# Placing a chunk's first DVE passes behind the scaling of transposes, and summing folded weights from PSUM, for three gates at once, with one copy no longer raised

## The chip, the cores and the metric

One core of one Trainium2 chip runs the whole program. The metric is the device time of one execution in microseconds (us). Several executions are quoted by their median, lowest and highest.

Names: TensorE (PE in the profile, PEld for its weight loads), VectorE (DVE), ScalarE (ACT), GpSimd (POOL), SyncE (SP, whose DMA issues are SPq). PSUM is the memory that TensorE writes to in this kernel, a bank one piece of it; SBUF is the memory of the other on-chip tiles.

Tiles in the profile: one unit of layer 0 makes, in this order, `pa` (adjacency times features), `ph` (times W1), `ps` (times W2) and `po` (adjacency again) in PSUM; `ag`, `hg`, `s` and `z` are what ACT makes of these four. `pT` is a transpose, `pf` a product of the fold, `parz` the first product of the loop of layer 3. A group such as `ps` stands for all its matmuls in one pass.

## The reference, cut to what matters

Four graph layers follow each other on `x` of shape (128, 64, 256) with one adjacency matrix of 64x64 per graph, each with a residual and a layer norm.

```python
# layer 0: five groups of nodes, two graph convolutions each (W1: 256->512, W2: 512->256)
x = _layernorm(x + _L0_gnn_ref(x, adj, W1, b1, W2, b2, fusion_w))
# layer 1: normalized adjacency, one matmul;  layer 2: polynomial in the row-normalized adjacency
x = _layernorm(x + _L1_gnn_ref(x, adj, W, b))
x = _layernorm(x + _L2_gnn_ref(x, adj, W, conv_w, conv_b))
# layer 3: five rounds of message passing and a GRU cell
x = _layernorm(x + _L3_gnn_ref(x, adj, nodemask, weight, w_ih, w_hh, b_ih, b_hh))

def _L3_gnn_ref(x, adj, mask, weight, w_ih, w_hh, b_ih, b_hh):
    A = (adj != 0).astype(x.dtype)
    h = x
    for l in range(5):
        m = jnp.einsum('bnd,de->bne', h, weight[l])
        agg = jnp.einsum('bij,bid->bjd', A, m)
        h = _gru_cell(agg, h, w_ih, w_hh, b_ih, b_hh)
    return h * mask[..., None]
```

## The kernel before

Layer 0 is worked in 16 units. While one unit multiplies, another is prepared: DVE builds a block-diagonal normalized adjacency `A`, TensorE transposes it into PSUM (`pT`), and DVE scales the transpose while it evicts it. The list `evictions` keeps these last scalings.

```python
        # prep(i), cut
                deg = small.tile([TR, w], F32, name="deg")
                nc.vector.tensor_reduce(deg[:r], av, AX.X, ALU.add)
                dinv = inv_sqrt(deg[:r], w, r, "d0")          # d0z, d0s on DVE; d0r on GpSimd; d0o on DVE
                nc.vector.tensor_mul(av, av, dinv[:, :, None].to_broadcast([r, w, u.n]))
                ...                                           # A0 = av * block, on DVE
                for t in range(ts.start, ts.stop):
                    nc.tensor.transpose(p[:r, t, :r], A0[:r, t, :r], ident[:r, :r])
                scale.append((AT[:r, ts, :r], p[:r, ts, :r], dinv[:, :, None].to_broadcast([r, w, r])))
            for v in scale:
                with tc.high_priority():
                    evictions.append(nc.vector.tensor_mul(*v))
```

Layers 1 and 2 take 8 graphs at a time (a chunk). Chunks 0 and 1 are woven into layer 0, the others into layer 3. A chunk's first stage reads the loaded adjacency `a64` twice, for `Ab` and for `rsum`; all the rest follows from these two.

```python
    def mid(c):
        a64 = adjs.pop(c)
        Ab = keep.tile([128, NP, 128], F32, name="Ab", bufs=1)
        nc.vector.tensor_mul(
            Ab.rearrange("p q (b m) -> p q b m", b=2),
            a64[:, :, None, :].to_broadcast([128, NP, 2, N]),
            pair[:, None, :, :].to_broadcast([128, NP, 2, N]),
        )
        A01 = keep.tile([128, NP, 128], F32, name="A01", bufs=4)
        nc.vector.tensor_scalar(A01, Ab, 0.0, None, op0=ALU.not_equal)
        rsum = small.tile([128, NP], F32, name="rsum")
        nc.vector.tensor_reduce(rsum, a64, AX.X, ALU.add)
        ...                                                   # rdeg, rinv, dinv1, dg from rsum
        nc.scalar.activation(poly, dg, AF.Identity, scale=cw[:, 2:3])
        ...
        yield
```

Between layer 0 and layer 3 the GRU's input weights are multiplied with each round's message weights (`pf`), and each product is split into the seven factors of a Strassen-like scheme (`V`; `WHH` for the hidden weights). Three copies on ACT and four sums on DVE belong to each product.

```python
    def factors(w, w21):
        nc.vector.tensor_add(w[:, 4, :], w21, w[:, 3, :])
        nc.vector.tensor_sub(w[:, 6, :], w[:, 0, :], w21)
        nc.vector.tensor_sub(w[:, 5, :], w[:, 4, :], w[:, 0, :])
        nc.vector.tensor_sub(w[:, 2, :], w[:, 1, :], w[:, 5, :])

    # fold(), cut: for each round l and gate q
                nc.scalar.copy(w[:, 0:2, :], p[:, :, 0:128])
                nc.scalar.copy(w[:, 3, :], p[:, 1, 128:256])
                v21 = ... work.tile([128, 128], F32, name="w21", bufs=3)
                nc.scalar.copy(v21, p[:, 0, 128:256])
                factors(w, v21)
                if l == 0:
                    factors(WHH[:, q], w21[:, q, :])

    # Chunk.state_of_layer2(k): the chunk's state transposed, first in the fold, later in the loop
            p = self.transpose(lambda q, k: self.xt[:, q, k * 128 : (k + 1) * 128], k, "pT3")
            with tc.high_priority():
                nc.scalar.copy(self.hT[:, k, :], p)
```

The build lays out each engine's queue. `tc.high_priority()` asks for an earlier place in it; `tc.issue_after(ins)` keeps an instruction behind `ins` in the queue (in the changed kernel `Ab` of chunk 0 runs at 174.69 us, behind the scaling at 169.20).

## Time and profile before

| | before |
|---|---|
| median of 3 runs | 2215.43 us (2214.81 to 2216.5) |
| profiled span | 2214.5 us, mean granted clock 0.994 |
| TensorE idle | 34.3 us, of which 15.1 us in one wait for `A` |

How to read it: TensorE is busy 98% of the span, so only what ends one of its few waits counts. The prediction shows the waits of TensorE, the timeline around the largest, and the windows with the clock. A number in square brackets at the end of a timeline line is how long the engine stood idle before that instruction, and what ended the idle time.

### The profile page before, as it was taken

How to read it: one execution, taken by the hardware profiler on the slowest of the kernel's cores; microseconds unless marked ns; L12 is line 12 of the kernel's file. 1: busy time of each engine (PE TensorE's matmuls, PEld its weight loads, DVE VectorE, ACT ScalarE, POOL GpSimd, SP SyncE). 2: the span in 40 equal slices, each digit the busy share in tenths (PEclk: the TensorE clock that was granted, in tenths of full speed). 3: DMA queues.
4: the chain of work that ended last, by engine and by line, in shares of the span. 5: the costliest groups of instructions: out<-in, count | busy, mean ns of one | idle time of the engine just before them, and what ended most of it. 6: DMA issues, size and time to landing. Idle time of an engine off the chain costs nothing.

```text
span 2214.5 us, 30166 instructions
## 1 busy us (share of the span) xinstructions
PE 2180.2 (98%) x11542; PEld 1911.4 (86%) x11542; DVE 1372.5 (62%) x3088; ACT 1003.1 (45%) x1853; POOL 571.0 (26%) x621
## 2 busy tenths in 40 slices
PE   9979999999999999999999999999999999999997
PEld 6657888888889889888889898888898898888886
DVE  3344666665766666666766676657666666566546
ACT  3233334445545454445454454455454544455453
POOL 3211122222222223223222222222222232232221
PEclk9989999999999999999999999999999999999999
DMA  5531210000100000000100010001000000000000
GB/s 166 178 109 55 58 46 4 1 3 1 41 1 4 1 20 22 3 1 7 35 1 3 1 41 1 3 1 41 1 1 1 20 10 1 1 10 11 1 1 20
DMA packets 54172, 51.12 MB, mean 23 GB/s; under 512 B 20878, under 2 KB 49036, under 8 KB 54028
## 3 DMA queue, kind: packets, MB, share of 16 engines
q1 hardware_dynamic: 49664, 43.96, 6.5%
q0 software_dynamic: 1936, 4.83, 0.8%
q8 instruction: 91, 1.49, 0.3%
q10 hardware_dynamic: 2428, 0.41, 0.1%
q14 instruction: 53, 0.43, 0.1%
HBM read 32.40 MB, written 16.78 MB: 22 GB/s over the span
## 4 chain that ended last, share of the span: by engine, by line
PE 94%; SPq 2%; DVE 1%; issue 1%; DMA 1%; ACT 0%; POOL 0%; POOLq 0%; DVEq 0%; ACTq 0%
PE parz L731 25%; PE pdrz L731 12%; PE pan L731 12%; PE pa L210 9%; PE pbrz L731 6%; PE pdn L731 6%; PE pT L772 4%; PE ps L442 4%; PE ph L426 3%; PE pbn L731 3%; PE pd L286 2%; PE pd L307 2%; SPq L362 1%; PE pa L411 1%; PE po L464 1%
## 5 line engine op out<-in xcount | busy, mean ns | idle before, releaser
L748 ACT COPY c<-parz 128x512 f32<-128x512 f32 x240 | 140.6, 586 | 322.4 <-PE parz L731 321.7
L731 PE MATMUL parz<-Th,WHH 128*128 128x256 f32 x960 | 286.0, 379 | 0.3 <-ACT c L748 0.3
L731 PE MATMUL parz<-Ta,V 128*128 128x256 f32 x960 | 285.8, 379 | 0.0
L711 POOL TENSOR_TENSOR Th<-hn 128x512 f32<-128x512 f32 x64 | 81.4, 1272 | 778.3 <-DVE hn L834 602.8
L831 ACT ACTIVATE NI<-NI,bih 128x512 f32<-128x512 f32 (+1 forms) x162 | 115.9, 715 | 206.0 <-DVE NI L826 205.8
L748 ACT COPY c<-pan 128x512 f32<-128x512 f32 x237 | 139.0, 586 | 150.1 <-PE pan L731 150.1
L731 PEld LDWEIGHTS parz<-Ta,V 128*128 128x128 f32 x960 | 182.5, 190 | 24.7
L731 PEld LDWEIGHTS parz<-Th,WHH 128*128 128x128 f32 x960 | 176.5, 191 | 21.1 <-ACT c L748 0.7
L803 ACT ACTIVATE RZ<-RZ,brz 128x512 f32<-128x512 f32 x160 | 116.0, 726 | 138.9 <-DVE RZ L760 138.9
L711 POOL TENSOR_TENSOR Ta<-agg 128x512 f32<-128x512 f32 x80 | 102.0, 1275 | 260.0 <-ACT agg L214 260.0
L760 DVE TENSOR_TENSOR RZ<-pdrz,c 128x512 f32<-128x512 f32 x80 | 55.0, 688 | 173.2 <-PE pdrz L731 173.2
L139 POOL TENSOR_TENSOR rs<-ve,mhalf 128x4 f32<-128x4 f32 (+3 forms) x67 | 68.9, 1029 | 298.3 <-DVE ve L137 234.4
L731 PE MATMUL pan<-Ta,V 128*128 128x256 f32 x474 | 141.3, 380 | 0.0
L731 PE MATMUL pan<-Th,WHH 128*128 128x256 f32 x474 | 141.1, 379 | 0.0
L754 DVE TENSOR_TENSOR NI<-pbn,c 128x512 f32<-128x512 f32 x79 | 54.6, 692 | 127.8 <-PE pbn L731 110.2
L210 PEld LDWEIGHTS pa<-A,h 128*128 128x128 f32 x1024 | 124.4, 192 | 3.3
L210 PE MATMUL pa<-A,h 128*128 128x128 f32 x1024 | 124.6, 275 | 0.0
L750 DVE TENSOR_TENSOR NI<-pdn,c 128x512 f32<-128x512 f32 x79 | 54.5, 689 | 112.7 <-ACT c L748 112.7
L832 DVE TENSOR_TENSOR RZ<-hn,NI 128x512 f32<-128x512 f32 (+1 forms) x129 | 87.8, 680 | 49.5 <-ACT NI L831 49.5
L834 DVE TENSOR_TENSOR hn<-RZ,NI 128x512 f32<-128x512 f32 (+1 forms) x161 | 109.8, 682 | 1.8
L833 DVE TENSOR_TENSOR RZ<-RZ 128x512 f32<-128x512 f32 (+1 forms) x161 | 109.5, 680 | 1.8
L442 PE MATMUL ps<-W,hg 128*125 128x256 f32 (+5 forms) x464 | 103.6, 380 | 0.3 <-ACT v L313 0.3
(220 smaller groups left out, 5077.0 us busy)
## 6 DMA issues: line engine op xcount, KB each, us to landing
out_dram<-xt SPq DMA_DIRECT2D x32, 256.0 KB
W<-in_w_dram SPq DMA_DIRECT2D x10, 512.0 KB
xt<-xb SPq DMA_DIRECT2D x32, 156.0 KB
xo<-in_x_dram SPq DMA_DIRECT2D x9, 512.0 KB
xb<-xo SPq DMA_DIRECT2D x9, 512.0 KB
xt<-xa SPq DMA_DIRECT2D x32, 100.0 KB
xg<-in_x_dram SPq DMA_DIRECT2D x25, 125.0 KB
xa<-xg SPq DMA_DIRECT2D x25, 125.0 KB
```

What stands on the lines that cost most here:

```text
L139: nc.gpsimd.tensor_tensor(rs[:r, :n], ve[:r, :n], mhalf[:r, :n], ALU.pow)
L210: nc.tensor.matmul(p[:, q * 128 : (q + 1) * 128], src[:, q, k * 128 : (k + 1) * 128], m[:, q, :], start=True, stop=True)
L442: nc.tensor.matmul(p[: u.rows[t], t - v, :], hg[:, e, u.off[t] : u.off[t] + u.rows[t]], W2[:, u.g, e, :], start=e == 0, stop=e == 3,)
L711: nc.gpsimd.tensor_sub(t[:, 0:2, :], a[:, :, H:], a[:, 0, :].rearrange("p (s n) -> p s n", s=2))
L731: nc.tensor.matmul(bank[:, g, :], w[:, q, i - 1, :], rhs, start=i in (1, 2, 5) and g == 0 and m == 0, stop=m == len(side) - 1, skip_group_ ...
L748: nc.scalar.copy(c, self.a)
L772: nc.tensor.transpose(p[:, q * 128 : (q + 1) * 128], src(q, k), ident)
L803: nc.scalar.activation(RZ[:, q, 0, :], RZ[:, q, 0, :], AF.Sigmoid, bias=b[0])
L831: nc.scalar.activation(n, n, AF.Tanh, bias=bih[:, 4 + j : 5 + j])
L832: e.tensor_sub(d, self.hT[:, j, f], n)
L833: e.tensor_mul(d, d, z)
L834: e.tensor_add(self.hn[:, j, f], d, n)
```

## The change

The intent: DVE should no longer reach `Ab` and `rsum` of the first chunk before their adjacency has landed. They are placed behind the most recent scaling of a transpose. In the fold, the sums with the fourth quarter of a product (`w21`) read it from the PSUM bank instead of a copy, the other sums of the three gates run in one instruction, and the copy of the transposed state (`hT`) loses its priority.

```diff
-        nc.vector.tensor_mul(
-            Ab..., a64..., pair...)
+        with tc.issue_after(evictions[-1].ins):
+            nc.vector.tensor_mul(
+                Ab..., a64..., pair...)
...
-        nc.vector.tensor_reduce(rsum, a64, AX.X, ALU.add)
+        with tc.issue_after(evictions[-1].ins):
+            nc.vector.tensor_reduce(rsum, a64, AX.X, ALU.add)
...
-    def factors(w, w21):
-        nc.vector.tensor_add(w[:, 4, :], w21, w[:, 3, :])
-        nc.vector.tensor_sub(w[:, 6, :], w[:, 0, :], w21)
-        nc.vector.tensor_sub(w[:, 5, :], w[:, 4, :], w[:, 0, :])
-        nc.vector.tensor_sub(w[:, 2, :], w[:, 1, :], w[:, 5, :])
+    def factors(w):
+        nc.vector.tensor_sub(w[:, :, 5, :], w[:, :, 4, :], w[:, :, 0, :])
+        nc.vector.tensor_sub(w[:, :, 2, :], w[:, :, 1, :], w[:, :, 5, :])
...
-                v21 = ... work.tile([128, 128], F32, name="w21", bufs=3)
-                nc.scalar.copy(v21, p[:, 0, 128:256])      # now for the last product alone
-                factors(w, v21)
-                if l == 0:
-                    factors(WHH[:, q], w21[:, q, :])
+                nc.vector.tensor_add(w[:, 4, :], p[:, 0, 128:256], w[:, 3, :])
+                nc.vector.tensor_sub(w[:, 6, :], w[:, 0, :], p[:, 0, 128:256])
+                if q == 2:
+                    factors(V[l])
+                if q == 2 and l == 0:
+                    nc.vector.tensor_add(WHH[:, :, 4, :], w21, WHH[:, :, 3, :])
+                    nc.vector.tensor_sub(WHH[:, :, 6, :], WHH[:, :, 0, :], w21)
+                    factors(WHH)
...
-            with tc.high_priority():
-                nc.scalar.copy(self.hT[:, k, :], p)
+            nc.scalar.copy(self.hT[:, k, :], p)
```

More of the change, by code (lines that the diff above doesn't have):

```diff
@@ L225, in mid @@
         Ab = keep.tile([128, NP, 128], F32, name="Ab", bufs=1)
-        nc.vector.tensor_mul(
-            Ab.rearrange("p q (b m) -> p q b m", b=2),
-            a64[:, :, None, :].to_broadcast([128, NP, 2, N]),
-            pair[:, None, :, :].to_broadcast([128, NP, 2, N]),
-        )
+        with tc.issue_after(evictions[-1].ins):
+            nc.vector.tensor_mul(
+                Ab.rearrange("p q (b m) -> p q b m", b=2),
+                a64[:, :, None, :].to_broadcast([128, NP, 2, N]),
+                pair[:, None, :, :].to_broadcast([128, NP, 2, N]),
+            )
         A01 = keep.tile([128, NP, 128], F32, name="A01", bufs=4)
@@ L675, in gnn_stack @@
     raw21 = []
-    def factors(w, w21):
-        nc.vector.tensor_add(w[:, 4, :], w21, w[:, 3, :])
-        nc.vector.tensor_sub(w[:, 6, :], w[:, 0, :], w21)
-        nc.vector.tensor_sub(w[:, 5, :], w[:, 4, :], w[:, 0, :])
-        nc.vector.tensor_sub(w[:, 2, :], w[:, 1, :], w[:, 5, :])
+    raw21 = []
+    def factors(w):
+        nc.vector.tensor_sub(w[:, :, 5, :], w[:, :, 4, :], w[:, :, 0, :])
+        nc.vector.tensor_sub(w[:, :, 2, :], w[:, :, 1, :], w[:, :, 5, :])
     def fold():
@@ L697, in fold @@
                 nc.scalar.copy(w[:, 3, :], p[:, 1, 128:256])
-                kept = l == L - 1 and q == 2
-                v21 = work.tile([128, 128], F32, name="kept21") if kept else work.tile([128, 128], F32, name="w21", bufs=3)
-                nc.scalar.copy(v21, p[:, 0, 128:256])
-                if kept:
+                if l == L - 1 and q == 2:
+                    v21 = work.tile([128, 128], F32, name="v21")
+                    nc.scalar.copy(v21, p[:, 0, 128:256])
                     raw21.append(v21)
-                factors(w, v21)
-                if l == 0:
-                    factors(WHH[:, q], w21[:, q, :])
+                nc.vector.tensor_add(w[:, 4, :], p[:, 0, 128:256], w[:, 3, :])
[6 more added lines that the diff above has]
+                    factors(WHH)
                 yield
```

## The prediction

> **What bounds the kernel now.** I read the page first (busy times, then the chain that ended last), then the waits of each engine, then the timeline around the two places where TensorE stood still.
>
> ```profile
> PE 2180.2 (98%) x11542; PEld 1911.4 (86%) x11542; DVE 1372.5 (62%) x3088; ACT 1003.1 (45%) x1853; POOL 571.0 (26%) x621
> PE 94%; SPq 2%; DVE 1%; issue 1%; DMA 1%; ACT 0%; POOL 0%; POOLq 0%; DVEq 0%; ACTq 0%
> ```
>
> The first line is the busy time of each engine in a span of 2214.5 us. TensorE is idle for 2214.5 - 2180.2 = 34.3 us in all. The change touches no matmul, so it can win from those 34.3 us and from slow clock, and from nothing else: 2% of 2215 us is 44 us, more than everything that is there. So the question is which part of the 34.3 us goes. The waits of TensorE say where most of it is (us in total, times, longest):
>
> ```profile
> PE pT L397 <- DVE A L389: 15.1, 1, 15.1
> PE pT L860 <- DVE hn L834: 4.1, 3, 1.6
> PE ph L426 <- ACT ag L416: 2.5, 1, 2.5
> PE pf L560 <- ACT w L700: 1.9, 1, 1.9
> PE pw L534 <- DVE zero L531: 1.5, 1, 1.5
> PE pa L411 <- DVE AT L401: 0.8, 1, 0.8
> ```
>
> One wait of 15.1 us holds nearly half. The rows pT L860 and pw L534 are the end and the start, which the change does not touch. From 350 to 2140 us, the long loop, TensorE has no gap (the windows view gives 1760.00 us of PE in the 1760 us from 380 to 2140). The timeline tells how the 15.1 us come about:
>
> ```profile
> 93.93 1.01 POOL L123 TENSOR_TENSOR d0r<-d0s,mhalf 126x4 f32<-126x4 f32 x1 [1.63 <-DVE d0s L121]
> 112.00 2.35 SPq L191 DMA_DIRECT2D a<-in_adj_dram  x2
> 119.25 0.69 DVE L226 TENSOR_TENSOR Ab<-a,pair 128x512 f32<-128x512 f32 x1 [25.46 <-DMA a<-in_adj_dram]
> 119.86 0.15 DVE L125 SCALAR_TENSOR_TENSOR d0o<-deg,d0r 126x4 f32<-126x4 f32 x1
> 120.68 0.75 DVE L389 TENSOR_TENSOR A<-ae,block 126x252 f32<-126x252 f32 x2
> 121.48 1.10 PE L397 MATMUL pT<-ident,A 126*126 126x126 f32 x4 [15.13 <-DVE A L389]
> 123.42 0.72 ACT L248 ACTIVATE poly<-dg,cw 128x512 f32<-128x512 f32 x1 [26.03 <-DVE dg L244]
> 124.65 0.65 ACT L416 COPY ag<-pa 128x264 f32<-128x264 f32 x2
> ```
>
> DVE works through a queue in order, and the queue has Ab of chunk 0 of the middle layers (L226, first used by TensorE at 213.69) in the middle of the preparation of layer 0's unit 7: behind d0s, ahead of d0o. The adjacency that Ab reads is issued by SP only at 112.00 and lands at 119.2. DVE stands for 25.46 us, d0o (its input from POOL was there at 94.94) and A wait behind, and TensorE, done with its work at 106.35, waits for A until 121.48. ACT has the same illness: poly, which needs dg of the same chunk, is ahead of ag, which makes the second wait (ph, 2.48 us). A third cost shows in the windows view (length, then PE, PEld, DVE, ACT, POOL busy, then clock, DMA share, GB/s):
>
> ```profile
> 100.00:106.00 6.00, 6.00 (x30) 5.20 (x28) 0.00 (x0) 0.00 (x0) 0.00 (x0) 1.00 0.40 96
> 115.00:120.00 5.00, 0.00 (x0) 0.00 (x0) 0.75 (x3) 0.00 (x0) 0.00 (x0) 0.50 0.43 111
> 125.00:127.00 2.00, 1.93 (x5) 1.52 (x6) 1.07 (x5) 1.27 (x4) 1.42 (x1) 0.50 0.43 160
> ```
>
> The granted clock is at half from 111 us until about 128, so that the first work after the stop also runs slow. The other place is the folding of weights, where TensorE waits 1.87 us:
>
> ```profile
> 323.32 0.58 ACT L780 COPY hT<-pT 128x512 f32<-128x512 f32 x1 [7.31 <-PE pT L772]
> 329.96 2.11 DVE L680 TENSOR_TENSOR WHH<-WHH,wh 128x128 f32<-128x128 f32 x2
> 338.18 1.99 PE L560 MATMUL pf<-ih,wl 128*128 128x256 f32 x8 [1.87 <-ACT w L700]
> ```
>
> hT, raised in priority, stands ahead of the fold's copies on ACT for 7.31 us while products from 317 us on are ready to be copied; and the sums on DVE, normally 0.28 us each, are stretched (two took 2.11).
>
> [...] L681 of 1.28 to 1.36 us ran beside L711 of POOL (1.37 us from 327.52). [...]
>
> **Part 1, Ab and rsum placed behind the last scaling of a transpose on DVE.** [...] By program order chunk 0's first stage is traced in the iteration after unit 11 was prepared, so Ab now follows AT of unit 11 (188.68 in the present trace), and chunk 1's follows AT of unit 14 (253.43). Both are far behind the landing at 119. So DVE runs d0o at 95, A by 96.5, and TensorE's transposes follow at 106 without a wait. What that is worth I take from the same work where it was not disturbed: unit 8 begins ps (32 matmuls of 256) at 150.23, pT at 157.24, ph (16 of 264) at 157.67, po at 161.24. That is 11.01 us from ps to po. In the disturbed pass ps begins at 99.18 and po at 130.22: 31.04 us. The difference is **20.0 us** (15.13 + 2.48 of waiting, some 2.4 of slow clock).
>
> Does the earlier work find its inputs? SP works off a backlog without a pause of note until 126, and that backlog does not move up. Unit 8's rows were issued by 96.5, needed at 148.31 - 20 = 128; unit 9's adjacency by 100.6, needed at 141.7 - 20 = 121.7; unit 10's by 119.1, needed at 160 - 20 = 140; unit 11's now waits for DVE and moves to about 126, needed at 153. All have 14 us or more, so I book no loss.
>
> What moves: about 3.5 us of DVE work for each of chunks 0 and 1. Chunk 0's has from about 169 to 193 (TensorE's transposes of Ab, 213.69 - 20). Chunk 1's has from 253.4 to 266.96 in present time, in which DVE has 3.9 us of plain idle before L314 and some gaps more. That fits narrowly, so I book **0.4 us** of new waiting around there.
>
> **Part 2, the fold.** Removed: 72 sums of 128x128 on DVE, 29 us busy in the trace (sum of L679 to L682) against 72 x 0.28 = 20 unblocked[...]; and 14 ACT copies of 0.28. Added: 30 sums with one input in PSUM, 128x128 (the PSUM form costs no more here: L754 0.69 against L832 0.68 at 512), and 14 sums of 128x384[...]. Measured start to start, 0.20 for the small (as 336.08 to 336.28)[...]. DVE gains little in plain time; it gains [...]that the ring of three w21 buffers, for which ACT waited 6.0 us, is gone. A bank is now held until DVE has read it, so DVE stays in TensorE's loop. I expect the wait of 1.87 to shrink to about 0.5: **1.4 us**.
>
> **Part 3, hT no longer raised.** In the fold it helps part 2. In the loop it happens 14 times; hT has some 14 us of other matmuls between its transposes and its first use by rz of the next step (eight products of 0.86 to 1.73 each), and an ACT copy in front costs 0.6 to 0.7 us. I book **0.2 us** lost.
>
> Sum: 2215.4 - 20.0 - 1.4 + 0.4 + 0.2 = **2194.6 us**.
>
> **The rivals.** (a) The wait is replaced: with DVE free, loads on the crowded SP queue hold TensorE up in 106 to 140 us. For it: SP issues without a break[...]. Against: the margins above. It would give back 3 to 10 us, 2198 to 2205. (b) The work put off collides with chunk 1's short window, or chunk 2's load, which SP must issue after Ab of chunk 0 has read its buffer, holds loads behind it in the SP queue. Against: the present trace has the same narrow order on a free DVE, and layer 0's loads are nearly all out by then. It would cost 1 to 6 us, about 2198. (c) Other order in the loop from ACT without the raised copies: a bank freed late, 14 times up to 0.5 us, 2200. (d) The fold's waits get worse, because a blocked large sum stands ahead of small ones that free banks: up to 3 us, 2197. A floor: 34.3 us idle plus 2.4 of slow clock, less some 12 us at the start and end: not under 2190.
>
> **Range and chances.** The trigger of the 20 us is plain and its removal certain, the rest is small on both sides, and rivals only lengthen: 2191 to 2202, with a tail upwards. Over 2% faster is out of reach (it needs 44 us), over 2% slower would need a new stall of 60 us, such as a queue in a bad order: 0.01 each way, 0.98 within.
>
> **What would show it.** Right: no wait of DVE for the adjacency, no row pT <- A and no ph <- ag among TensorE's waits, clock 1.00 between 110 and 128, PE busy lower by some 2 us with the same count, po of unit 5 near 110 and all later work 20 us earlier; Ab after 168; the row pf <- w gone, a smaller one to DVE in its place. Wrong: a new wait of TensorE of over 2 us before 200 (a), near 240 to 260 (b), at each change of chunk (c) or in the fold (d).

## The result, and the profile after

The changed kernel took 2195.51 us (median of 4 runs, 2195.18 to 2197.59), against 2215.97 us of the kernel before beside it (4 runs, 2214.81 to 2217.66). The ratio is 0.9909, 95% interval 0.9892 to 0.9926: within 2%. All ratios here are the mean time of one kernel's runs over that of the other's in the same rounds, so they are not quite the ratio of the medians.

Busy times of the engines, and the chain that ended last by engine, in the changed kernel:

```profile
PE 2177.2 (99%) x11542; PEld 1907.7 (87%) x11542; DVE 1362.9 (62%) x3060; ACT 1001.2 (46%) x1839; POOL 571.2 (26%) x621
PE 96%; DVE 1%; issue 1%; POOL 0%; ACT 0%; DMA 0%; SPq 0%; POOLq 0%; ACTq 0%; DVEq 0%
```

SPq, 2% of the chain before, is at 0%. TensorE idles 2193.5 - 2177.2 = 16.3 us instead of 34.3. Its waits in the changed kernel (us in total, times, longest), to be held against the rows that the prediction quotes:

```profile
PE pT L865 <- DVE hn L839: 4.1, 3, 1.6
...
PE pT L778 <- DVE V L705: 0.9, 1, 0.9
...
PE ph L428 <- ACT ag L418: 0.5, 1, 0.5
```

The rows of 15.1 and 2.5 us are gone (the 0.5 of ph lies at 12.39 us, at the start). In the fold, 0.9 us remain of 1.9. The same pass in the timelines, first of the kernel before and then of the changed kernel:

```profile
99.18 7.17 PE L442 MATMUL ps<-W,hg 128*126 128x256 f32 x32
...
130.22 1.95 PE L464 MATMUL po<-AT,s 126*128 126x126 f32 x16
```

```profile
95.54 0.16 DVE L125 SCALAR_TENSOR_TENSOR d0o<-deg,d0r 126x4 f32<-126x4 f32 x1 [1.19 <-POOL d0r L123]
95.95 0.75 DVE L391 TENSOR_TENSOR A<-ae,block 126x252 f32<-126x252 f32 x2
99.74 7.17 PE L444 MATMUL ps<-W,hg 128*126 128x256 f32 x32
106.75 0.60 PE L399 MATMUL pT<-ident,A 126*126 126x126 f32 x4
107.18 3.73 PE L428 MATMUL ph<-ag,W 128*128 128x264 f32 x16
110.75 1.95 PE L466 MATMUL po<-AT,s 126*128 126x126 f32 x16
111.80 2.25 SPq L191 DMA_DIRECT2D a<-in_adj_dram  x2
...
174.69 0.66 DVE L227 TENSOR_TENSOR Ab<-a,pair 128x512 f32<-128x512 f32 x1
```

The load is issued when it was before (111.80 against 112.00), but nothing stands behind it: `A` is built at 95.95, ten us before TensorE wants it, and `Ab` runs at 174.69, long after the landing and without a wait. The windows from 106 to 130 us (length, then busy time and count of PE, PEld, DVE, ACT, POOL, then clock, DMA share, GB/s), before and after:

```profile
106.00:130.00 24.00, 6.39 (x22) 4.74 (x21) 7.80 (x38) 4.29 (x9) 3.82 (x3) 0.64 0.49 150
```

```profile
106.00:130.00 24.00, 24.00 (x119) 17.09 (x118) 13.43 (x65) 10.05 (x18) 4.38 (x5) 1.00 0.51 163
```

TensorE is busy throughout and the clock stays at 1.00. From the starts of the same TensorE groups in both timelines the whole difference can be laid out, by stages (us; each is a difference of two starts in one timeline):

| stage | before | after | difference |
|---|---|---|---|
| span's start to ps of this pass | 99.18 | 99.74 | +0.56 |
| ps to po of this pass | 31.04 | 11.01 | -20.03 |
| po to the first product of the fold (pf) | 185.07 | 185.13 | +0.06 |
| fold: first pf to first matmul of the loop (parz) | 33.85 | 32.78 | -1.07 |
| loop: first parz to last transposes (pT) | 1856.66 | 1856.19 | -0.47 |
| last pT to the span's end | 8.69 | 8.69 | 0.00 |
| sum | 2214.48 | 2193.54 | -20.94 |

Such stages are free of the noise of the start and serve for the experiments too.

### The profile page after: what moved, and what is told of

It reads as the page before. It is cut to its first block, busy times and chain, and to the rows that moved or that the text cites.

```text
span 2193.5 us, 30145 instructions
## 1 busy us (share of the span) xinstructions
PE 2177.2 (99%) x11542; PEld 1907.7 (87%) x11542; DVE 1362.9 (62%) x3060; ACT 1001.2 (46%) x1839; POOL 571.2 (26%) x621
## 4 chain that ended last, share of the span: by engine, by line
PE 96%; DVE 1%; issue 1%; POOL 0%; ACT 0%; DMA 0%; SPq 0%; POOLq 0%; ACTq 0%; DVEq 0%
PE parz L737 25%; PE pdrz L737 12%; PE pan L737 12%; PE pa L210 9%; PE pbrz L737 6%; PE pdn L737 6%; PE ps L444 4%; PE ph L428 4%; PE pT L778 4%; PE pbn L737 3%; PE pd L288 3%; PE pd L309 2%; PE pa L413 1%; PE po L466 1%; PE pf L562 1%
```

## The experiments

Each kernel is judged beside runs of the kernel before on the same chip. Those had medians of 2214.84 us (first four), 2213.85 (next four) and 2215.94 (last two).

The theory: (1) nearly all of the gain is that late data no longer stands at the head of DVE's queue; (2) about one us comes from the fold, by the sums from the bank; (3) the copy of hT without priority costs a little in the loop. The rivals: the gain comes from the fold; one of the two placements is enough; it is slow clock more than waiting; it is the position in the queue and not the lateness of the data; the fold's gain is that of hT.

### Part 1 alone

```diff
 (before)
+        with tc.issue_after(evictions[-1].ins):   # around Ab, and around rsum
```

> The kernel before with part 1 alone: Ab and rsum placed behind the last scaling of a transpose on DVE; fold and hT as before. My theory: this part carries nearly the whole gain, 20.0 us, so 2196 us; no wait of DVE for the adjacency, no wait pT <- A; the fold's wait pf <- w stays at about 1.9 us. Rival (the fold's sums or the lower priority of hT carry a good part): 2200 us or more here.

It took 2196.35 us (2196.09 to 2197.9), ratio 0.9916 (0.9899 to 0.9933). The wait for `A` is gone, and the fold's wait is still there:

```profile
PE pf L562 <- ACT w L702: 1.8, 1, 1.8
```

Part 1 alone gives 18.5 us between the medians (2214.84 - 2196.35), where the whole change gave 20.5 beside other runs. The stages tell it without the noise of the start: from ps to po it takes 11.01 us, as in the changed kernel, so all of the 20.03 us there is part 1. Its fold stage lasts 33.79 us, as before.

### All but part 1

```diff
 (before)
+  the new fold, and hT without priority; Ab and rsum as before
```

> The changed kernel with Ab and rsum put back without the placing: the new fold and the unraised hT alone. My theory: the wait pT <- A of 15.1 us is back, the fold's wait falls from 1.9 to about 0.9, so 1 us less than before: 2214.5 us. Rival (the fold and hT carry a good part): 2211 us or less.

It took 2213.25 us (2211.73 to 2217.75), ratio 0.9994 (0.9978 to 1.0009): not told apart from the kernel before. Waits of TensorE, largest first:

```profile
PE pT L397 <- DVE A L389: 13.0, 1, 13.0
...
PE pT L776 <- DVE V L703: 0.9, 1, 0.9
```

The stall stays, 2 us shorter because in this run DVE could use the load 1.4 us earlier (Ab at 117.83 us instead of 119.25) and TensorE came to it 0.7 us later (ps at 99.85 instead of 99.18). The fold's wait is 0.9 and its stage 32.77 us. Both parts do what they do independently of each other. The gain does not come from the fold.

### Ab placed, rsum left

```diff
 (before)
+        with tc.issue_after(evictions[-1].ins):   # around Ab alone
```

> The kernel before with Ab placed behind the last scaling, but rsum left free. rsum reads the same load, and it now stands in Ab's place in DVE's queue, between d0s and d0o of unit 7. My theory (an instruction that waits for the late load blocks the queue, whichever it is): the wait pT <- A is still 14 to 15 us, and the time 2213 to 2216 us. Rival (it is the size of Ab, or the DVE work put off with it, that counts): at least half of the gain, 2206 us or less.

It took 2222.59 us (2219.76 to 2224.51), ratio 1.0032 (1.0017 to 1.0046): slower than before, and slower than I expected. The timeline of this kernel:

```profile
118.89 0.42 DVE L235 TENSOR_REDUCE rsum<-a 128x4 f32<-128x256 f32 x1 [24.28 <-DMA a<-in_adj_dram]
121.58 0.72 ACT L249 ACTIVATE poly<-dg,cw 128x512 f32<-128x512 f32 x1 [25.99 <-DVE dg L245]
122.21 0.66 ACT L431 ACTIVATE hg<-ph,b 128x504 f32<-128x504 f32 x1
122.92 8.48 PE L443 MATMUL ps<-W,hg 128*126 128x256 f32 x26 [21.36 <-ACT hg L431]
```

DVE stands for the same load, now with `rsum` in the place of `Ab`: placing one of two readers moves the stall to the other. It is longer for TensorE because the rest of the order changed as well. ACT's poly, which needs dg and so rsum, now has its place ahead of an hg that was ready, and TensorE waits 21.36 us for that hg, in the middle of ps, instead of 15.13 us for `A`. I had expected the wait to stay at pT and at 14 to 15 us; that missed. Not all of the extra time is the stall. By stages, ps to po takes 35.24 us against 31.04, 4.2 us more; the fold takes 35.53 against 33.85, though its code is the same and so is its wait (1.86 us against 1.87). Here the 8 matmuls after that wait took 3.48 us instead of 1.99. I put that down to slow clock, as an estimate: at a clock of 0.50 four transposes of the kernel before took 1.10 us (121.48) where the changed kernel's took 0.60 at 1.00 (106.75), and the mean granted clock of this run is 0.992 against 0.994. In the kernel before the clock stayed at 1.00 from 336 to 344 us. On both engines ready work stood behind the instruction that waited: on DVE d0o ran at 119.22, 0.33 us after rsum, though its input from GpSimd was there at 95.76; on ACT hg started 0.63 us after poly, after 25.99 us in which ACT did nothing.

### Useless matmuls in the stall

```diff
 (before)
+                if i == 7 and ts.start == 0:
+                    f = psum0("pfill")
+                    for _ in range(16):
+                        nc.tensor.matmul(f, W1[:, 1, 0, :128], W1[:, 1, 0, :], start=True, stop=True)
                 for t in range(ts.start, ts.stop):
                     nc.tensor.transpose(...)
```

> The kernel before with 16 useless matmuls (128x128 by 512, to a bank that nobody reads) put on TensorE ahead of the transposes of unit 7, where it waits 15.1 us. They take about 14 us and so should be hidden in the wait; they keep the clock up. My theory (the gain of 20.0 us is 17.6 of waiting and 2.4 of slow clock): the time falls by 1.5 to 2.4 us although TensorE does more work, to about 2213 us; granted clock 1.00 from 106 to 128. Rival (the slow clock costs nothing on the path, the 20.0 are waiting alone): unchanged at 2215 to 2216, or longer.

The output is unchanged, since no one reads the bank. It took 2211.24 us (2209.92 to 2211.77), ratio 0.998 (0.9966 to 0.9995). I had expected about 2213. The clock stayed at 1.00 from 106 to 130 us. The timeline:

```profile
107.03 13.90 PE L400 MATMUL pfill<-W 128*128 128x512 f32 x32
120.76 0.60 PE L402 MATMUL pT<-ident,A 126*126 126x126 f32 x4
...
124.76 1.95 PE L469 MATMUL po<-AT,s 126*128 126x126 f32 x16
```

From pT to po this takes 124.76 - 120.76 = 4.00 us, as in the changed kernel (110.75 - 106.75 = 4.00). In the kernel before it took 130.22 - 121.48 = 8.74, of which 2.48 was the wait for ag; so slow clock cost 8.74 - 2.48 - 4.00 = **2.26 us**. The clock was at half there for 17.1 us (111.0 to 128.1), but TensorE worked in only 4.15 us of them (121.48 to 128.11, less the wait of 2.48). The total is not a clean measure. In the profiled run the load landed 4 us earlier (Ab at 115.17 us), and the filler overran the moment at which `A` was ready. So the clock is the small part of the stall, and keeping TensorE busy is no substitute for ending the wait.

### The load 30 us earlier, the first readers not placed

```diff
 (before)
-    load_adj(c) for c in (0, 1) on SP, at unit g0
+    load_adj(c, nc.gpsimd) for c in (0, 1), with the loads of the weights, some 30 us earlier
+    Ab and rsum placed for the later chunks only; fold and hT as before
```

> The kernel before with the cause of the wait taken away in another way: the adjacency of chunks 0 and 1 is loaded some 30 us earlier, from GpSimd's queue, and their Ab and rsum stay as early on DVE as the build puts them (now ahead of unit 6's scaling); only chunks 2 and on are placed behind the last scaling, so that no other late load stands in front. Fold and hT as before. My theory (DVE stood for a load that came late): the 15.1 us go here too, at the price of up to 4 us where Ab waits for its new load: 2196 to 2200 us. Rival (it is the early place of the work on DVE that costs, not the waiting for data): 2205 us or more.

It took 2198.31 us (2196.35 to 2200.19), ratio 0.9926 (0.9911 to 0.9941). The first two chunks were not placed behind a scaling, and the stall is gone all the same: DVE waits 4.0 us for the adjacency, TensorE has no wait for `A`, and ps to po takes 11.01 us. In DVE's queue they did not stay where they were: the build put `Ab` of chunk 0 ahead of unit 6's scaling (86.22 us, before AT at 92.62), earlier still than in the kernel before. An even earlier place costs no stall once the data is there. So it is the lateness of the data and not the early place that costs; placing is the cheaper cure. From ps to the first pf it takes 195.82 us here, against 196.14 in the changed kernel, 0.32 us less: putting the chunks' work off has a small price. This version loses more than that at its start (ps only at 101.83 us, with 1.3 us of waiting for an ag at 14.48 us and 0.7 for the load of `ident`) and keeps the old fold (33.86 us).

### The fold and hT crossed

Two kernels with part 1, one with the new fold and hT still raised, one with the old fold and hT not raised:

```diff
 (after)                                       e6
-            nc.scalar.copy(self.hT[:, k, :], p)
+            with tc.high_priority():
+                nc.scalar.copy(self.hT[:, k, :], p)
```

> The changed kernel with hT raised in priority again: part 1 and the new fold. The fold's wait of TensorE is 0.9 us in the changed kernel. If the sums from the bank and the three gates at once are what shortened it, it stays at 1 us or less. If it was the unraised hT (which lets the fold's copies start while the transposes are still to come), it is back at about 1.9 us or more. Time 2195 to 2197 us either way.

```diff
 (after)                                       e7
-  the new fold
+  the old fold: w21 copied by ACT, four sums of 128x128 for each product
```

> The other corner: part 1 and the unraised hT, with the old fold (72 sums of 128x128, w21 copied by ACT into three buffers). If the unraised hT is what shortened the fold's wait, it is 1 us or less here; if the new sums are, it is 1.9 us or about. I hold it for mixed: 1 to 1.5. Time 2195 to 2197 us either way. In the loop, where hT is copied 14 times, I expect no wait of TensorE at the changes of chunk.

Their times are 2196.91 us (2196.16 to 2197.08) and 2195.78 us (2195.35 to 2196.33). The waits of TensorE in the fold, first with hT raised and the new sums, then with hT not raised and the old sums:

```profile
PE pf L562 <- DVE V L705: 2.0, 1, 2.0
```

```profile
PE pf L562 <- ACT w L702: 0.8, 1, 0.8
```

With the first and the second experiment's numbers this makes a square (TensorE's wait in the fold; in brackets the fold stage from the first pf to the first parz):

| | old fold | new fold |
|---|---|---|
| hT raised | 1.8 (33.79) | 2.0 (33.90) |
| hT not raised | 0.8 (32.82) | 0.9 (32.78) |

**The whole us comes from hT.** The new sums give nothing on the path with either order. I had held e7 for mixed, 1 to 1.5 us; that missed. Each cell is one profiled run, but others repeat it: with hT not raised the stage took 32.77 to 32.84 us in all six profiled runs, and the kernel before and the one with the early load, with hT raised and the old sums, took 33.85 and 33.86. Two kernels with hT raised fall outside: the one with Ab alone placed (35.53, with the 8 slow matmuls told above) and the one with the useless matmuls (33.12, a wait of 1.2). In the last one the queue was laid out with ACT's copies of three products (from 311.88 us) ahead of hT (317.94), so ACT did not stand for it. It is thus hT's place in ACT's queue that costs, which the priority asks for but does not fix. Why it costs is plain from ACT's timeline with hT raised and the new sums:

```profile
304.51 0.58 ACT L786 COPY hT<-pT 128x512 f32<-128x512 f32 x1 [7.31 <-PE pT L778]
```

ACT stands 7.31 us for a transpose that comes late, with finished products in front of it, exactly as in the kernel before. All that follows the copies is late by that, whether there are four sums to a product or two.

### The bank sums with priority

```diff
 (after)
+                with tc.high_priority():
                     nc.vector.tensor_add(w[:, 4, :], p[:, 0, 128:256], w[:, 3, :])
                     nc.vector.tensor_sub(w[:, 6, :], w[:, 0, :], p[:, 0, 128:256])
```

> A try at a better version: the changed kernel with the two sums that read the bank raised in priority, so that on DVE they go ahead of the last normalizations of layer 0, behind which they now wait while TensorE waits 0.9 us for their bank. My theory (bank held until DVE has read it): the wait of 0.9 us goes, the time falls by up to 0.9 us, to about 2194.6, which the rounds may not resolve. Rival (the normalizations that are pushed back hold up something else): the same or longer.

It took 2195.68 us (2194.72 to 2197.87), and the wait stayed at 0.9 us (fold stage 32.79). DVE kept its order, the normalization of layer 0's last unit ahead of the first bank sum. The timeline of the changed kernel shows that order:

```profile
297.85 0.37 ACT L698 COPY V<-pf 128x256 f32<-128x256 f32 x1 [1.25 <-PE pf L562]
304.61 0.92 DVE L154 TENSOR_SCALAR xg<-xg,mv,rs 125x256 f32<-125x256 f32 x2 [0.61 <-POOL rs L139]
305.45 0.28 DVE L704 TENSOR_TENSOR V<-pf,V 128x128 f32<-128x128 f32 x1
306.47 0.63 PE L778 MATMUL pT<-ident,xt 128*128 128x128 f32 x4 [0.87 <-DVE V L705]
```

ACT copies from the first product at 297.85, but DVE reads from it only at 305.45, after the normalization. Until then the bank is not free, and TensorE waits for it. Why the priority did not move the sums stays open.

### The first three products copied by ACT

To free the early banks without DVE, ACT copies `w21` of the first round's three products; the others are summed from the bank. The changed kernel itself ran again beside it.

```diff
 (after)
+                v21 = p[:, 0, 128:256]
...
+                elif l == 0:
+                    v21 = work.tile([128, 128], F32, name="w21", bufs=3)
+                    nc.scalar.copy(v21, p[:, 0, 128:256])
+                nc.vector.tensor_add(w[:, 4, :], v21, w[:, 3, :])
+                nc.vector.tensor_sub(w[:, 6, :], w[:, 0, :], v21)
```

> A second try at a better version, from what the earlier runs showed: in the changed kernel TensorE waits 0.9 us for a bank of the first layer's products, because DVE, which must read it, is still at the last normalizations of layer 0. Here the first layer's three products are copied whole by ACT (three buffers, each used once), so ACT alone frees those banks; the other twelve are summed from the bank as in the changed kernel. My theory: the wait pT <- V goes and no other takes its place, 0.9 us less than the changed kernel run beside it. Rival: the wait only moves on to a later bank, because DVE then stands for the load of WHH (3.2 us in the changed kernel): the sum of TensorE's waits in the fold stays at 0.8 us or more and the time is the same.

> The changed kernel once more, unaltered, beside the version with the first products copied and against the kernel before on the same chip: 2195 to 2196 us, 0.9 us longer than that version if the theory of it holds, equal if the rival does. It also shows whether the wait of 0.9 us in the fold and the absence of a wait in layer 0 repeat.

It took 2196.26 us (2195.83 to 2197.19), the changed kernel 2195.34 us (2195.02 to 2197.54, 5 runs), with 0.9 us of waiting in the fold as at first. With the three copies the wait has not shrunk but moved, from 306 us to a later bank:

```profile
307.89 2.48 DVE L684 TENSOR_TENSOR V<-V 128x384 f32<-128x384 f32 x1
307.89 0.76 POOL L693 DMA_DIRECT2D WHH<-in_whhT_dram  x1
311.64 0.56 DVE L714 TENSOR_TENSOR WHH<-WHH,wh 128x384 f32<-128x384 f32 x1 [1.27 <-DMA WHH<-in_whhT_dram]
318.33 1.97 PE L562 MATMUL pf<-ih,wl 128*128 128x256 f32 x8 [0.89 <-DVE V L709]
```

A large sum with both inputs in SBUF took 2.48 us instead of 0.55, and then DVE stood 1.27 us for the load of `WHH`; the small bank sums wait behind both. The long sum started at the same 307.89 us as a DMA issue of GpSimd (0.76) and ended after GpSimd's next subtraction (1.27, from 308.67); in the changed kernel the same sum, 0.03 us ahead of the same issue, took 0.54. It is one case, and no run explains it. DVE's order in the fold has more than one late head, and the banks now hang on it. From 311.64 us to past 318 its timeline lists one pause, of 0.18 us. So the rival that the expectation named held: the wait moved. None of the nine other kernels beat the changed one by more than the spread of its runs.

## Why the prediction was right, and where it was not

The predicted 2194.6 us lies 0.9 us under the median, and the range held. By its steps:

- **Part 1, 20.0 us: right, 20.03 measured**, from ps to po, at exactly the 11.01 us that the undisturbed pass had promised. It held because the estimate took the same work where nothing disturbed it, and did not add up causes. The causes fit as well: 15.13 and 2.48 of waiting, and 2.26 of slow clock against the predicted 2.4. The clock, at half from 111.0 us, was full again at 128.1, 3.0 us after the ph matmuls began at 125.07. One reading beside it does not come out of the trace: only a single L681 sum was as long as said, 1.36 us. The fifth experiment shows that it is the lateness of the data, the third that both readers of the late data have to be placed.
- **New waiting near chunk 1, 0.4 us lost: right in kind, 0.27 in size.** From the po before it to chunk 1's transposes of Ab it takes 3.84 us (243.92 to 247.76) instead of 3.57 (263.39 to 266.96); in the fifth experiment, where this chunk is not put off, 3.57 again. The timeline of the changed kernel shows the way it takes:

```profile
245.37 1.02 ACT L315 ACTIVATE v<-pd,cb,rinv 128x256 f32<-128x256 f32 x2 [1.95 <-DVE xt L317]
246.28 1.43 ACT L470 ACTIVATE z<-po,gb,gw 128x500 f32<-128x500 f32 x2
247.76 0.42 PEld L259 LDWEIGHTS pT<-ident,Ab 128*128 128x128 f32 x4 [0.30 <-ACT z L470]
```

  DVE is late with xt, having the put-off chunk in its queue just before (its dg runs at 240.44); ACT's v waits for DVE, z stands behind v, and TensorE waits for the bank that z reads. Over the whole stretch from po to the fold the net loss was only 0.06 us, since the kernel before had a wait of its own here: 0.19 us at 278.02 for poly, after chunk 2's Ab and the work around it at 269.64. That one is not in the changed kernel, and I had not counted on it.
- **Part 2, 1.4 us from the fold: the step that failed.** The fold gave 1.07 us, but none of it from the sums: with hT raised, the new sums left a wait of 2.0 us. The prediction said that the ring of `w21` and the stretched sums made the wait; it named hT in the same view and booked it as a mere help. Crossed, hT gives all of it. On DVE itself part 2 turns 72 sums into 44, and 29.2 us busy into 17.7; the bank sums were never longer than 0.29 us, even beside GpSimd (0.28 at 311.56, within a subtraction of 1.46 from 311.31), and the unhindered sums of 128x384 took 0.55. That DVE would gain little in plain time was my estimate, and why the old sums were stretched beside GpSimd was not shown. All that is off the path. ACT stood for a late transpose, and no speed of what comes after it could matter.
- **Part 3, 0.2 us lost in the loop: not there.** The loop takes 1856.19 us both with hT raised (part 1 alone) and without (changed kernel). The kernel before had 1856.66 in its profiled run, but the kernel with the useless matmuls has the old loop and the old order and shows 1856.19. So the 0.47 us that the stages show in the loop cannot be credited to the change: they are two delays of 0.20 us at 610.85 and 0.26 us at 846.22, each at a matmul that reads poly, which came in that one run and not in the others.
- **Rivals.** (a), the SP queue: no such wait, TensorE busy throughout from 106 to 130 (in the kernel before SP did pause between 106 and 126, for 0.77 us at 119.60 and 1.74 at 120.74). (b), the collision with chunk 1: 0.27 us, not 1 to 6. (c), the loop: nothing. (d), large sums ahead of small ones: not visible in the time of the changed kernel, though the last experiment shows that very thing as soon as the first wait is taken away.
- **The rest of the distance.** Between the two spans lie 20.9 us, against 20.8 predicted; between the medians 20.5. The start of a run moves by more than the error: ps began between 99.18 and 102.24 us in the profiled runs, with other small waits at the start. The kernel before spreads from 2212.35 to 2219.31 us over all its runs, the changed one from 2195.02 to 2197.59. That fits the cause: the old stall ended with a load, and DVE could use that load at 119.25, 117.83 and 115.17 us in three profiled runs of the same load order.

What repeats in the runs is 20.03 - 0.06 + 1.07 = 21.04 us. That this lies so near 20.8 is sound for part 1, which is 95% of it, and luck for the rest: the sums were put at 1.4 us and gave none, hT was put at a loss of 0.2 us and gave 1.07, and the two errors nearly cancel.

## What to carry to other kernels

When an engine stands for a load, look at what ready work stands behind it in its queue, take the gain from the same work where it ran undisturbed, and place every reader of the late data: with one left, the stall went to that one and the run was 7.8 us slower than before. When two edits meet in one short stage, cross them and measure that stage from start to start; the total time of a run cannot tell 1 us of 2200. Work saved on DVE was worth nothing here while ACT, which feeds it, stood for something late at the head of its own queue.
